# The last LayerNorm's scaling on ScalarE, the floor of the degrees on GpSimd, and a later store

## The chip, the cores and the metric

The kernel runs on one core of one Trainium2 chip. The metric is the device time of one execution in microseconds (us), as the median of seven. One further execution was taken with the hardware profiler; its page and its trace are what the text reads. Engines: PE is TensorE (PEld its weight loads), DVE is VectorE, ACT is ScalarE, POOL is GpSimd, SP is SyncE, which here only issues DMAs.

## What is computed

128 graphs of 128 nodes with 512 features each go through two layers. Layer 0 is graph attention with 8 heads of 64 features; layer 1 is a hypergraph convolution with a hidden width of 1024, a LayerNorm, and a second hypergraph convolution. Each layer adds its input and is followed by a LayerNorm without weights. The reference, cut to what matters:

```python
def _layernorm(x, axis=-1, eps=1e-5):
    m = jnp.mean(x, axis=axis, keepdims=True)
    v = jnp.var(x, axis=axis, keepdims=True)
    return (x - m) / jnp.sqrt(v + eps)

# layer 0, per graph and head
dense = leaky_relu(e_self[:, None] + e_neigh[None, :], 0.2) + NEG_BIG * (1.0 - A)
out = softmax(dense) @ feats + b          # heads side by side, then relu

# layer 1
def hypergraph_conv(x, adj, W, b):
    H = (adj != 0); w = adj.reshape(N, -1)[:, :C]
    xw = x @ W.T
    Dn = H @ w;         Dn = where(Dn > 0, 1 / Dn, 0)
    Be = H.sum(axis=1); Be = where(Be > 0, 1 / Be, 0)     # the degrees
    return Dn * (H @ (Be * (H.T @ xw))) + b
h = layer_norm(relu(hypergraph_conv(x, adj, W1, b1)), gamma, beta)
y = hypergraph_conv(h, adj, W2, b2) + x

x = _layernorm(x + layer0(x, adj))
x = _layernorm(x + layer1(x, adj))        # the last LayerNorm
```

## The kernel before

All arithmetic is in float32. Two graphs form a pair (index p, 64 pairs; g = 0, 1 within one), and most tiles hold both. A pair passes through five stages of one period each, so that five pairs are in work at a time. Every piece of work is a function registered with a lag (which period after the pair's start) and a time within a period of T = 38.6; the number `(p + lag) * T + time` is its place in one list. The list is sorted, and each engine and each DMA queue gets its instructions in this order[...]. For the first pairs a dictionary `first` sets places by hand, for the last two pairs there are others. The place numbers only order the work; real time is set by the engines.

The steps that the prediction speaks of, in the order of a pair:

- `edges` (L401, lag 0): DVE turns the adjacency block by block, makes the 0/1 matrix hT and sums its rows into deg (L411), takes the maximum of deg and 1 (L415) and the reciprocal (L416). deg has 2 numbers in each of the 128 partitions. `scale_edges` (L420, lag 1): DVE multiplies hT by the reciprocal into hB (L423). `propagator` (L428) multiplies hB and hT on PE, `r_evict` (L438) scales the result by the nodes' degrees into R (L440).
- `spread_rows` (L528): the neighbours' scores go from ft through DRAM (rd, L542); `neighbours` (L550, L560) spreads them to all partitions as nb (two loads of 512 KB), `spread_nodes` (L563, L566) the nodes' degrees as dnb.
- `masked` (L576, L579): POOL adds the mask to the scores, in four quarters; `leaky` (L583, L595) on ACT; `largest` (L597, L601) on DVE; `exponential` (L606, L609) on ACT. The exponentials go through DRAM to be transposed (L613, L621, L630), `attend` multiplies on PE, `attended`, `add_bias` (POOL, L691) and `residual` (DVE, L698) finish layer 0.
- The first LayerNorm: `moments` (L701) and `rstds` (L709) give mean (mv) and 1/sqrt (rs; vea and rsa for the first, veo and rso for the last LayerNorm), with the power on POOL (L714). `first_shift` (L727) makes -mean * rs on ACT in three small instructions (L730, L732), `first_output` (L737) scales on ACT with it (L739).
- `propagate` (pz on PE, L762), `z_evict` (ACT, zT, L774), `z_sums` (POOL, zS, L785), `hidden` (PE, ph, L797), with copies of partial products by ACT (L332); `h_sum`, `relu`, `square`, and `squares` (POOL, L850), which adds the squares of the hidden LayerNorm in three steps for each g; `h_sums` (POOL, hS, L458); `weigh` on PE (py, L476).
- The hidden LayerNorm's sums go through DRAM as well: `sum_blocks` (DVE), `write_sums` (SP, sd, L906), `read_sums` (SP, L912), `sum_rest` (DVE, L920, L922), `h_rstd` (POOL, L946 to L949, veh and rsh), `y_scale` (DVE, L953).
- `skip` (DVE, L750) starts o, `output` (PE, pq, L963), `o_sum` (DVE, L972), `o_stats` (DVE, L706), `rstds` with key "o"; `o_norm` (L984, lag 4, 17.0) calls `normalize` (L716), which takes (o - mean) * rs on DVE for each g (L717); `store` (L989, L990, lag 4, 19.5) writes o. o has two buffers.

SP issues nearly all DMAs of the steady part, in the order of the list. Around the store that is: the rows of x in blocks (L121), the store (L990), the adjacency in blocks (L129), rd (L542), nb (L560, twice), dnb (L566), sd (L906), the next rows of x (L112), the sums (L912, four), the next adjacency (L98, L104).

The very last pair has its own tail (`last_norm` and others, L994 to L1084), with its normalization on DVE.

Of the kernel before, what the change touches and what calls it, by code (L numbers as in the profile page):

```python
# [8 lines left out]
F32 = mybir.dt.float32  # L9
AF = mybir.ActivationFunctionType  # L10
ALU = mybir.AluOpType
# [9 lines left out]
def kernel(  # L21
# [45 lines left out]
    nc = tc.nc  # L67
    G, N, F = x.shape
    P = 128
# [15 lines left out]
    small = ctx.enter_context(tc.tile_pool(name="small", bufs=4))  # L85
# [114 lines left out]
    for i in range(2):  # L200
        t = const.tile([P, 2, H, UW + 1], F32, name=f"ft{i}")
# [99 lines left out]
    LAST = PAIRS - 1  # L301
    steps = []

    def step(lag, time, since=0, until=PAIRS):

        def keep(fn):
            steps.append((lag, time, fn.__name__, range(since, until), fn, ()))
            return fn
        return keep

    def at(lag, time, fn, *args, since=0, until=PAIRS):
        steps.append((lag, time, fn.__name__, range(since, until), fn, args))
# [87 lines left out]
    @step(0, 35.75)  # L400
    def edges(p, s):  # L401

        deg = small.tile([P, 2], F32, tag="deg", name=f"deg_{p}")
        hT = work.tile([P, 2, N], F32, tag="hT", name=f"hT_{p}")
        if p < 2:
            src = s["pt"][:, :2 * N].rearrange("p (g n) -> p g n", g=2)
        else:
            src = hT
            nc.vector.transpose(hT.rearrange("p g (b n) -> p (g b) n", b=NB), s["ab"])
        for g in range(2):  # L410
            nc.vector.tensor_scalar(  # L411
                hT[:, g, :], src[:, g, :], 0.0, None, op0=ALU.not_equal, op1=ALU.add,
                accum_out=deg[:, g:g + 1],
            )
        nc.vector.tensor_scalar(deg, deg, 1.0, None, op0=ALU.max)  # L415
        nc.vector.reciprocal(deg, deg)  # L416
        s["hT"], s["be"] = hT, deg

    @step(1, 10.8)
    def scale_edges(p, s):  # L420
        s["hB"] = work.tile([P, 2, N], F32, tag="hB", name=f"hB_{p}")
        for g in range(2):
            nc.vector.tensor_scalar(  # L423
                s["hB"][:, g, :], s["hT"][:, g, :], s["be"][:, g:g + 1], None, op0=ALU.mult
            )
# [287 lines left out]
        s["rs", key] = small.tile([P, 2], F32, tag="rs", name=f"rs{key}_{p}")  # L713
        nc.gpsimd.tensor_tensor(s["rs", key], ve, mhalf, op=ALU.pow)  # L714

    def normalize(s, key, t, g):  # L716
        nc.vector.tensor_scalar(  # L717
            t, t, s["mv", key][:, g, 0:1], s["rs", key][:, g:g + 1], op0=ALU.subtract,
            op1=ALU.mult,
        )  # L720

    at(2, 26.2, residual, 0)
    at(2, 30.7, residual, 1)
    at(2, 30.8, rstds, "a")

    @step(2, 33.12)
    def first_shift(p, s):  # L727
        s["sh"] = small.tile([P, 2], F32, tag="sh", name=f"sh_{p}")
        nm = small.tile([P, 2], F32, tag="nmean", name=f"nmean_{p}")
        nc.scalar.activation(nm, s["mv", "a"][:, :, 0], AF.Identity, scale=-1.0)  # L730
        for g in range(2):
            nc.scalar.activation(  # L732
                s["sh"][:, g:g + 1], nm[:, g:g + 1], AF.Identity,
                scale=s["rs", "a"][:, g:g + 1],
            )

    def first_output(p, s, g):  # L737
        t = s["y"][:, g, :]
        nc.scalar.activation(  # L739
            t, t, AF.Identity, bias=s["sh"][:, g:g + 1], scale=s["rs", "a"][:, g:g + 1]  # L740
        )

    at(2, 33.13, first_output, 0)
    at(2, 33.14, first_output, 1)

    def skip(p, s, g):
# [119 lines left out]
    def weigh(s, i, to, start):  # L866
# [3 lines left out]
          QU, 1, until=LAST)  # L870
# [109 lines left out]
    at(4, 15.5, o_stats, 1, until=LAST)  # L980
    at(4, 15.6, rstds, "o", until=LAST)

    @step(4, 17.0, until=LAST)
    def o_norm(p, s):  # L984
        for g in range(2):
            normalize(s, "o", s["o"][:, g, :], g)

    @step(4, 19.5, until=LAST)
    def store(p, s):  # L989
        nc.sync.dma_start(out[2 * p:2 * p + 2].rearrange("g n f -> n g f"), s["o"])  # L990

# [80 lines left out]
    for t, fn, *args in (  # L1072
# [40 lines left out]
        ("nodes", 0): 12.9, ("write_nodes", 0): 12.92, ("spread_nodes", 0): 15.9,  # L1113
        ("edges", 0): 14.46, ("edges", 2): 119.2,
        ("x_transpose", 2, 0): 120.5, ("x_transpose", 2, 1): 121.1, ("scale_edges", 0): 14.47, ("propagator", 0): 14.55,
        ("r_evict", 0): 99.76,
        ("spread_rows", 1): 15.72, ("nodes", 1): 15.55, ("write_nodes", 1): 15.85,
        ("edges", 1): 110.4, ("scale_edges", 1): 110.5, ("neighbours", 1): 80.1,
        ("propagator", 1): 117.76, ("spread_nodes", 1): 80.3, ("r_evict", 1): 121.8,
# [98 lines left out]
```

## Time and profile before

| | |
|---|---|
| median of 7 executions | 2461.6 us (2461.19 to 2462.88) |
| the profiled execution | 2461.45 us, of which the span from first to last instruction is 2459.4 us |
| granted PE clock | 0.998 |
| PE, steady part (200 to 2350 us) | busy 2146.84 of 2150 us |
| DMA | 345.30 MB, mean 140 GB/s |

In the steady part a pair takes some 37.6 us. Views of the profile used below: the page gives each engine's busy time and the share of the span; groups list instructions by line, engine and shapes ("xcount | busy us, mean ns | idle before"); waits list "engine line waited for <- releaser: us in total, times, longest"; timelines give start, length, engine, line, operation and, in brackets, the idle time before and what ended it. A busy PE is not a PE at its peak, and a wait is put down to what came last by the profile.

The groups that the change touches:

| line | what | count | mean |
|---|---|---|---|
| L717 | DVE, normalization of o, 128x512 | 126 | 772 ns |
| L415 | DVE, maximum of deg and 1, 128x2 | 64 | 996 ns |
| L416 | DVE, reciprocal of deg, 128x2 | 64 | 166 ns |
| L739 | ACT, scaling of the first LayerNorm, 128x512 | 128 | 799 ns |
| L730, L732 | ACT, its shifts, 128x2 and 128x1 | 64, 128 | 203, 287 ns |
| L990 | SP, the store, 512 KB | 63 | 407 ns to issue (median) |

### The profile page before, as it was taken

Reading aid. Unit: us, or ns where it says so; the run is one execution under the profiler, and the core shown is the slowest. Engines: PE = TensorE matmul, PEld = TensorE weight load, DVE = VectorE, ACT = ScalarE, POOL = GpSimd, SP = SyncE. Lnnn points to the kernel's source line nnn. Section 1 sums busy time; section 2 is a strip of 40 time slices with the busy share of each in tenths; the row PEclk is TensorE's granted clock in tenths of the full one; section 3 lists DMA queues with packets and bytes.
Section 4 is the critical chain, followed back from the end, with each engine's and each line's share of the span. In section 5 each row is a group of like instructions: output and inputs, shape, how many; then the busy total and the mean of one; then the engine's idle time right before and its main releaser. Section 6 shows DMA issues by size and latency. Waiting matters only on the chain.

```text
span 2459.4 us, 53018 instructions
## 1 busy us (share of the span) xinstructions
PE 2427.1 (99%) x18273; PEld 2148.7 (87%) x18273; DVE 2021.9 (82%) x4580; ACT 1532.3 (62%) x4481; POOL 1825.8 (74%) x2060
## 2 busy tenths in 40 slices
PE   7999999999999999999999999999999999999998
PEld 5888888888888888888888888888888888888897
DVE  7988888888888888888888888888888888888876
ACT  4665665755756656657557566566575665665763
POOL 5877777777777777777777777777777778777774
PEclk9999999999999999999999999999999999999999
DMA  6545445445454454454454544554545545545531
GB/s 183 142 141 144 146 132 154 143 128 152 140 141 144 142 144 145 130 155 141 130 153 139 142 144 143 146 145 129 152 142 133 151 138 144 143 140 150 144 111 52
DMA packets 432763, 345.30 MB, mean 140 GB/s; under 512 B 153176, under 2 KB 382064, under 8 KB 432496
## 3 DMA queue, kind: packets, MB, share of 16 engines
q1 hardware_dynamic: 429024, 337.46, 48.2%
q10 hardware_dynamic: 3472, 4.47, 0.5%
q8 instruction: 145, 2.38, 0.4%
q14 instruction: 122, 1.00, 0.1%
HBM read 239.08 MB, written 102.73 MB: 139 GB/s over the span
## 4 chain that ended last, share of the span: by engine, by line
PE 50%; DVE 19%; POOL 18%; ACT 6%; issue 4%; DMA 3%; SPq 0%; POOLq 0%; DVEq 0%; ACTq 0%
PE phX L797 10%; PE pyX L476 9%; POOL hS L458 6%; PE pfX L476 5%; PE phW L797 5%; PE pyW L476 5%; POOL zS L785 3%; POOL sq L850 3%; ACT nb L595 3%; PE pav L667 3%; PE pz L762 2%; PE phY L797 2%; DVE y L953 2%; PE pq L963 2%; PE pfW L476 2%
## 5 line engine op out<-in xcount | busy, mean ns | idle before, releaser
L797 PEld LDWEIGHTS phX<-zS,w_sb 128*128 128x128 f32 x3072 | 363.1, 192 | 33.0 <-issue 31.6
L332 ACT COPY py<-pyX 128x257 f32<-128x257 f32 x189 | 70.6, 374 | 506.6 <-PE pyX L476 503.9
L797 PE MATMUL phX<-zS,w_sb 128*128 128x128 f32 x3072 | 374.3, 275 | 2.4 <-POOL xS L458 1.3
L850 POOL TENSOR_TENSOR sq<-sq 128x512 f32<-128x512 f32 (+2 forms) x384 | 343.2, 894 | 20.1
L579 POOL TENSOR_TENSOR nb<-nb,neg 128x512 f32<-128x512 f32 x256 | 318.4, 1277 | 7.3 <-DMA nb<-rd 7.3
L609 ACT ACTIVATE nb<-nb,nm 128x128 f32<-128x128 f32 x1024 | 318.0, 391 | 8.1 <-DVE nm L601 8.1
L595 ACT ACTIVATE nb<-nb,ft 128x128 f32<-128x128 f32 x1020 | 317.2, 388 | 7.1 <-POOL nb L579 7.1
L714 POOL TENSOR_TENSOR rso<-veo,mhalf 128x2 f32<-128x2 f32 x63 | 44.1, 700 | 371.2 <-DVE veo L712 371.2
L827 ACT ACTIVATE h<-h,vecs 128x128 f32<-128x128 f32 x768 | 245.1, 392 | 55.2 <-DVE h L812 55.2
L601 DVE TENSOR_REDUCE nm<-nb 128x4 f32<-128x512 f32 x256 | 174.6, 682 | 113.2 <-ACT nb L595 101.3
L476 PE MATMUL pyX<-w_sb,hS 128*128 128x257 f32 x1008 | 245.6, 385 | 0.0
L476 PE MATMUL pyX<-w_sb,h 128*128 128x257 f32 x1008 | 239.4, 379 | 0.5 <-ACT py L332 0.5
L476 PE MATMUL pyW<-w_sb,hS 128*128 128x256 f32 x1008 | 238.7, 379 | 1.0 <-DVE y L881 1.0
L476 PEld LDWEIGHTS pyW<-w_sb,hS 128*128 128x128 f32 x1008 | 190.6, 189 | 29.0 <-POOL rsa L714 1.7
L476 PEld LDWEIGHTS pyX<-w_sb,hS 128*128 128x128 f32 x1008 | 185.8, 189 | 28.6
L691 POOL TENSOR_TENSOR y<-y,b_bc 128x512 f32<-128x512 f32 x128 | 163.2, 1275 | 61.6 <-DVE y L682 61.6
L476 PEld LDWEIGHTS pyX<-w_sb,h 128*128 128x128 f32 x1008 | 186.4, 190 | 25.5 <-ACT py L332 0.9
L698 DVE SCALAR_TENSOR_TENSOR y<-y,x 128x512 f32<-128x512 f32 x128 | 153.6, 1200 | 56.7 <-POOL y L691 55.1
L667 PEld LDWEIGHTS pav<-ft,eT 128*64 128x64 f32 x4096 | 130.0, 138 | 43.8 <-issue 41.9
L953 DVE SCALAR_TENSOR_TENSOR y<-y,rsh,bw_bc 128x512 f32<-128x512 f32 x126 | 148.6, 1217 | 21.1 <-POOL rsh L949 19.8
L630 DVE STREAM_TRANSPOSE eT<-eb 128x512 f32<-128x512 f32 x252 | 163.5, 687 | 0.3 <-DMA eb<-ed 0.2
L838 ACT ACTIVATE sq<-h 128x512 f32<-128x512 f32 x256 | 160.5, 628 | 2.1
(174 smaller groups left out, 5747.2 us busy)
## 6 DMA issues: line engine op xcount, KB each, us to landing
nb<-rd SPq DMA_DIRECT2D x127, 512.0 KB
ed<-nb SPq DMA_DIRECT2D x126, 512.0 KB
eb<-ed SPq DMA_DIRECT2D x504, 128.0 KB
x<-in_x_dram SPq DMA_DIRECT2D x64, 512.0 KB
out_dram<-o SPq DMA_DIRECT2D x63, 512.0 KB
xb<-in_x_dram SPq DMA_DIRECT2D x248, 128.0 KB
a<-in_adj_dram SPq DMA_DIRECT2D x64, 128.0 KB
w<-in_adj_dram SPq DMA_DIRECT2D x128, 64.0 KB
```

Of the source, the lines that this page charges most:

```text
L476: nc.tensor.matmul(to[:, :n], lhs[:, k, :], rhs[:, k, :n], start=bool(start) and k == 0, stop=(k == nk - 1), skip_group_check=True,)
L579: nc.gpsimd.tensor_tensor(t, t, neg[:, :, None, :].to_broadcast([P, NB, HH, B]), op=ALU.add)
L595: nc.scalar.activation(t, t, AF.Prelu, bias=s["ft"][:, g, h, 0:1], alpha=SLOPE)
L601: nc.vector.tensor_reduce(s["nm"][:, g, hs], scores(p, s, g, hs).rearrange("p b h j -> p h b j"), AX.XY, ALU.max, negate=True,)
L609: nc.scalar.activation(t, t, AF.Exp, bias=s["nm"][:, g, h:h + 1])
L630: nc.vector.transpose(s["eT"][:, g, hs, :].rearrange("p h (b i) -> p h b i", b=NB), s["eb", g][:, :, hs, :].rearrange("p b h j -> p h b j"),)
L667: nc.tensor.matmul(t[rows, h * (U + 1):(h + 1) * (U + 1)], s["eT"][:, g, q * HH + h, rows], s["ft"][:, g, q * HH + h, 2:], start=True, sto ...
L691: nc.gpsimd.tensor_tensor(s["y"][:, g, :], s["y"][:, g, :], b0_bc, op=ALU.add)
L797: nc.tensor.matmul(to[:, m * N:(m + 1) * N], w[:, k, m * P:(m + 1) * P], rhs[:, k, :], start=bool(start) and m == 0 and k == 0, stop=(k == ...
L827: nc.scalar.activation(dst[:, k, :], src[:, k, :], AF.Relu, bias=b1_sb[:, c:c + 1])
L850: nc.gpsimd.tensor_tensor(t[:, :n, :], t[:, :n, :], t[:, n:2 * n, :], op=ALU.add)
L953: nc.vector.scalar_tensor_tensor(t, t, s["rs", "h"][:, g:g + 1], bw_bc.rearrange("p (j c) -> p j c", j=2), op0=ALU.mult, op1=ALU.add,)
```

## The change

The normalization of o by the last LayerNorm (all pairs but the last) goes from DVE to ACT, in the form that the first LayerNorm has: three small instructions for the shift, then a scaling for each g. Its place goes from 17.0 to 21.3, 21.4 and 23.5 in the period, behind the last of the squares (21.2); the second half stands behind the copy of the features (23.4). The store goes from 19.5 to 28.5, behind rd, nb and dnb and ahead of sd. The maximum of the degrees and 1 becomes a step of its own on POOL (`least_degree`, lag 0, 36.0, and by hand for the first three pairs), in place; the reciprocal stays on DVE and moves from `edges` to the head of `scale_edges`.

```diff
--- before.py
+++ after.py
@@ -412,12 +412,15 @@
                 hT[:, g, :], src[:, g, :], 0.0, None, op0=ALU.not_equal, op1=ALU.add,
                 accum_out=deg[:, g:g + 1],
             )
-        nc.vector.tensor_scalar(deg, deg, 1.0, None, op0=ALU.max)
-        nc.vector.reciprocal(deg, deg)
         s["hT"], s["be"] = hT, deg
+
+    @step(0, 36.0)
+    def least_degree(p, s):
+        nc.gpsimd.tensor_scalar(s["be"], s["be"], 1.0, None, op0=ALU.max)
 
     @step(1, 10.8)
     def scale_edges(p, s):
+        nc.vector.reciprocal(s["be"], s["be"])
         s["hB"] = work.tile([P, 2, N], F32, tag="hB", name=f"hB_{p}")
         for g in range(2):
             nc.vector.tensor_scalar(
@@ -713,32 +716,30 @@
         s["rs", key] = small.tile([P, 2], F32, tag="rs", name=f"rs{key}_{p}")
         nc.gpsimd.tensor_tensor(s["rs", key], ve, mhalf, op=ALU.pow)
 
-    def normalize(s, key, t, g):
-        nc.vector.tensor_scalar(
-            t, t, s["mv", key][:, g, 0:1], s["rs", key][:, g:g + 1], op0=ALU.subtract,
-            op1=ALU.mult,
-        )
-
     at(2, 26.2, residual, 0)
     at(2, 30.7, residual, 1)
     at(2, 30.8, rstds, "a")
 
     @step(2, 33.12)
     def first_shift(p, s):
-        s["sh"] = small.tile([P, 2], F32, tag="sh", name=f"sh_{p}")
-        nm = small.tile([P, 2], F32, tag="nmean", name=f"nmean_{p}")
-        nc.scalar.activation(nm, s["mv", "a"][:, :, 0], AF.Identity, scale=-1.0)
+        shifts(p, s, "a")
+
+    def shifts(p, s, key):
+        sh = s["sh", key] = small.tile([P, 2], F32, tag="sh", name=f"sh{key}_{p}")
+        nm = small.tile([P, 2], F32, tag="nmean", name=f"nmean{key}_{p}")
+        nc.scalar.activation(nm, s["mv", key][:, :, 0], AF.Identity, scale=-1.0)
         for g in range(2):
             nc.scalar.activation(
-                s["sh"][:, g:g + 1], nm[:, g:g + 1], AF.Identity,
-                scale=s["rs", "a"][:, g:g + 1],
+                sh[:, g:g + 1], nm[:, g:g + 1], AF.Identity, scale=s["rs", key][:, g:g + 1]
             )
 
+    def shifted(s, key, t, g):
+        nc.scalar.activation(
+            t, t, AF.Identity, bias=s["sh", key][:, g:g + 1], scale=s["rs", key][:, g:g + 1]
+        )
+
     def first_output(p, s, g):
-        t = s["y"][:, g, :]
-        nc.scalar.activation(
-            t, t, AF.Identity, bias=s["sh"][:, g:g + 1], scale=s["rs", "a"][:, g:g + 1]
-        )
+        shifted(s, "a", s["y"][:, g, :], g)
 
     at(2, 33.13, first_output, 0)
     at(2, 33.14, first_output, 1)
@@ -980,12 +981,17 @@
     at(4, 15.5, o_stats, 1, until=LAST)
     at(4, 15.6, rstds, "o", until=LAST)
 
-    @step(4, 17.0, until=LAST)
-    def o_norm(p, s):
-        for g in range(2):
-            normalize(s, "o", s["o"][:, g, :], g)
-
-    @step(4, 19.5, until=LAST)
+    @step(4, 21.3, until=LAST)
+    def o_shift(p, s):
+        shifts(p, s, "o")
+
+    def o_norm(p, s, g):
+        shifted(s, "o", s["o"][:, g, :], g)
+
+    at(4, 21.4, o_norm, 0, until=LAST)
+    at(4, 23.5, o_norm, 1, until=LAST)
+
+    @step(4, 28.5, until=LAST)
     def store(p, s):
         nc.sync.dma_start(out[2 * p:2 * p + 2].rearrange("g n f -> n g f"), s["o"])
 
@@ -1113,7 +1119,8 @@
         ("nodes", 0): 12.9, ("write_nodes", 0): 12.92, ("spread_nodes", 0): 15.9,
         ("edges", 0): 14.46, ("edges", 2): 119.2,
         ("x_transpose", 2, 0): 120.5, ("x_transpose", 2, 1): 121.1, ("scale_edges", 0): 14.47, ("propagator", 0): 14.55,
-        ("r_evict", 0): 99.76,
+        ("r_evict", 0): 99.76, ("least_degree", 0): 14.465, ("least_degree", 1): 110.45,
+        ("least_degree", 2): 119.25,
         ("spread_rows", 1): 15.72, ("nodes", 1): 15.55, ("write_nodes", 1): 15.85,
         ("edges", 1): 110.4, ("scale_edges", 1): 110.5, ("neighbours", 1): 80.1,
         ("propagator", 1): 117.76, ("spread_nodes", 1): 80.3, ("r_evict", 1): 121.8,
```

## The prediction, made before the changed kernel had run

> **What bounds the kernel now.** I read the busy times of the page first, then the waits of the steady part (200 to 2350 us), then the timelines of ACT and PE over two neighbouring pairs. Two lines of the page:
>
> ```profile
> PE 2427.1 (99%) x18273; PEld 2148.7 (87%) x18273; DVE 2021.9 (82%) x4580; ACT 1532.3 (62%) x4481; POOL 1825.8 (74%) x2060
> PEclk9999999999999999999999999999999999999999
> ```
>
> PE has work all the time at full clock. Time can be lost only in the few places where it waits, and can be gained only there or in the ramp. The waits of the steady part, most of which concern other engines:
>
> ```profile
> POOL rso L714 <- DVE veo L712: 334.4, 57, 5.9
> POOL zS L785 <- ACT zT L774: 49.0, 57, 1.1
> PEld phX L797 <- ACT zT L774: 8.7, 29, 0.3
> ACT zT L774 <- PE pz L762: 8.3, 28, 0.3
> DVE so L920 <- DMA sums_out<-sd: 10.2, 12, 2.2
> ```
>
> The third line is PE's whole loss that is not its own issue: 0.3 us in every second pair. The timelines show why (start, length):
>
> ```profile
> 1224.28 0.59 ACT L774 COPY zT<-pz 128x512 f32<-128x512 f32 x1 [0.30 <-PE pz L762]
> ...
> 1261.20 1.11 ACT L774 COPY zT<-pz 128x512 f32<-128x512 f32 x2
> ...
> 1224.08 2.01 PE L797 MATMUL phX<-zT,w_sb 128*128 128x128 f32 x16
> ...
> 1261.83 2.05 PE L797 MATMUL phX<-zT,w_sb 128*128 128x128 f32 x16
> ...
> 1299.32 2.00 PE L797 MATMUL phX<-zT,w_sb 128*128 128x128 f32 x16
> ```
>
> From phX to phX the two intervals are 37.75 and 37.49 us, of which the tightest that PE alone would need is about 37.44. From the end of the second zT copy (1224.87) to the end of the next one (1262.31) is 37.44 too. That second interval is a loop without PE, and the chain of waits follows it: zT, POOL's zS sums and rsh, then DVE without a gap from L953 to veo (L712), POOL's rso, squares L850, hS L458 and bias L691, DVE's L698 and vea, POOL's rsa, ACT's first_output and leaky, zT. In the first pair zT waits 0.30 us for PE; in the next PE waits for zT. So a longer loop costs its extra once in two pairs (about 31 times), and a shorter one gives at most the 0.3 us back, 31 times: 9.3 us.
>
> [...]
>
> ```profile
> L415 DVE TENSOR_SCALAR deg<-deg 128x2 f32<-128x2 f32 x64 | 63.7, 996 | 2.2
> L353 DVE TENSOR_SCALAR dn<-dd 128x2 f32<-128x2 f32 x64 | 12.7, 198 | 2.2
> L717 DVE TENSOR_SCALAR o<-o,mvo,rso 128x512 f32<-128x512 f32 x126 | 92.3, 772 | 0.0
> L416 DVE RECIPROCAL deg<-deg 128x2 f32<-128x2 f32 x64 | 10.6, 166 | 2.2
> ```
>
> The same two-element operation takes 996 ns beside POOL's mask additions (L579) and 198 beside an idle POOL. [...]
>
> **Normalization from DVE to ACT.** DVE loses 2 x 772 = 1.54 us a pair. It stood at 1203.0 to 1204.5 in the pair of 1200; behind it DVE does L499 and then idles 1.16 us until ACT's pf copy, and 0.37 us for POOL's L691 at 1211.2. So DVE's own time there is worth nothing. But it held up POOL's squares, which are in the loop: L850 takes 0.795 us (256 wide) and 0.520 (128 wide) beside L717, against 0.73 for zS of the same 256 columns and 0.452 for the 128-wide sum of g = 1. Gain to the loop: 0.065 + 0.068 = 0.13 us. ACT gets one L730 (203 ns), two L732 (287) and two L739 (799), some 2.2 us with overlaps. It has the square until 1206.48 and the ft copy at 1207.74, then nothing until 1210.37. The shifts and the first half end near 1207.8 and may push the ft copy by 0 to 0.1 us; the second half is done by 1208.5. DVE's rows transpose that needs ft starts at 1209.16. Cost 0; without that idle time it would be up to 2.2 us a pair. The statistics are ready since 1202.1, so ACT waits for nothing.
>
> **Floor of the degrees, reciprocal.** DVE loses L415 (0.996) and, there, L416 (0.166). What follows is R (L440) and the score maxima L601, and the waits put 89.6 us of L601 down to ACT's leaky: DVE arrives earlier and waits, gain 0. On POOL the floor costs what L947, also a 128x2 tensor_scalar, does: 222 ns. It stands between the mask additions (end 1223.94) and zS (1224.94, after 1.00 us of idling for zT; 0.68 in the next pair), and deg is ready at 1220.4: cost 0 in the steady part. If that gap were gone, 0.3 us in the loop. The reciprocal moves into scale_edges, between L750 and L423, and there DVE is in the loop with no gap: 0.165 + 0.034 until the dependent L423 = +0.20 us. Bounds for the loop in all: +0.20 if the squares gain nothing, -0.1 if they gain twice what I read. Taken: 0.20 - 0.13 = +0.07, x 31 = **+2.2 us** (-3 to +6.2).
>
> **The ramp.** The hand-made times of the first pairs put least_degree(2) at 119.25, on POOL between the second zS sum of pair 0 (119.2) and the third (119.9). In the trace:
>
> ```profile
> 57.25 0.73 POOL L785 TENSOR_TENSOR zS<-zT 128x256 f32<-128x256 f32 x1
> 57.94 0.73 POOL L785 TENSOR_TENSOR zS<-zT,zS 128x256 f32<-128x256 f32 x1
> 58.63 1.27 POOL L579 TENSOR_TENSOR nb<-nb,neg 128x512 f32<-128x512 f32 x1
> ...
> 61.91 1.27 ACT L595 ACTIVATE nb<-nb,ft 128x128 f32<-128x128 f32 x4
> 63.08 0.57 ACT L332 COPY ph<-phX 128x512 f32<-128x512 f32 x1
> ```
>
> DVE finishes the degrees of pair 2 at 60.67. POOL, in order, would stand from 57.3 to then. Behind it are two sums and the last mask addition of pair 1: 60.75 + 0.30 + 0.73 + 0.69 + 1.27 = 63.7. ACT's leaky of that quarter moves from 61.91 to 63.75, and behind it in ACT's order the copy of ph, for which PE waits already (63.79): +1.84 us. Earlier, least_degree(1) stands on POOL behind two mask additions (to 52.59), where DVE now has L423 at 50.18; L423, two short L423 against POOL's third addition, then L237: DVE is 0.4 to 0.8 us later, of which 0.45 reaches the degrees of pair 2. Sum **+2.3 us**; 0 if the later waits of the ramp (PE waits 1.00 us at 91.5 and 0.66 at 95.9) swallow it, 3 at most. The floor of pair 0 stands before a 6 us idle stretch of POOL: 0.
>
> **The store.** SP around it, in a usual pair:
>
> ```profile
> 1129.73 0.41 SPq L990 DMA_DIRECT2D out_dram<-o  x1
> ...
> 1135.66 0.94 SPq L560 DMA_DIRECT2D nb<-rd x2
> ```
>
> SP's later issues there: dnb 1136.65, sd 1140.85, x 1141.23, sums_out 1144.99. The store, 512 KB, moves behind dnb and so ahead of sd, x and the reading of the sums. SP itself has 3.7 us free between dnb and sd, so 0.41 us of issuing costs nothing. In the queue the store puts its transfer before sd: 1.4 us at the 300 GB/s seen at 1144 to 1145, 3 us if shared. DVE takes the sums at 1149.08, just as they land; POOL needs veh only after zS, 3.5 us later, 3.0 after DVE's two instructions. Behind L920 on DVE stand one L601 and the h sum L812, which begins 3.7 us later. Cost 0 in the usual pair. Some pairs are short of slack (in the pair of 1200 the wait at L920 is already 1.4 us, and sd took 5.1 us instead of 3.3): I take **+1 us** in all (0 to 5). nb stays ahead of the store; the o buffer is next written 19 us later.
>
> **Sum.** The profiled execution took 2461.45 us (span 2459.4, 2.05 around it), 0.15 below the median. 2461.45 + 2.2 + 2.3 + 1 = 2466.95, say **2467**. Its own range is 2462 to 2473.
>
> **Rivals.**
> - The loop shortens (not slower): [...] the net loop is 0.3 us shorter. PE's wait disappears: 2461.45 - 9.3 + 2.3 = 2454.5. It ends faster by more than a measurement can tell once the loop is 0.24 us shorter. [...] Against: the squares at 1239.82 show only the 0.13.
> - The store decides (slower): sd lands more than 3.0 us later and the sums hold up veh, DVE's L953 and the loop in each pair. At 0.5 us over, x 60 pairs: 2462 + 30 = 2492. For it: a store beside others took some 3 us, and L920 has no slack of its own. Against: 1.4 us at full rate and 3 us of slack to veh.
> - Nothing measurable: ramp swallowed, loop even: 2462.
>
> **How the numbers follow.** Forecast 0.52, shorter loop 0.15, store 0.17, nothing 0.16. About 0.2 % (4.9 us) is what can be told from no change here. A third of the forecast's case lies within it, all of the last: faster 0.15, same 0.34, slower 0.51. The range takes the forecast's own, the last rival, a third of the first and half of the store's: 2457 to 2477.
>
> **What would show it.** PE's wait for zT: 8.7 us now, about 11 by my sum, gone if the first rival is right. L850 at 0.73 and 0.45 behind rso; L423 0.2 us later after L750; POOL idle from 57.3 to 60.7 and PE's phX at 65.6 instead of 63.79; L920 waiting in most pairs but rsh never behind it. I am wrong if PE waits for y of L953 (store), or if ACT's ft copy or py copies come late.

## The result, and the profile after

The changed kernel takes 2467.7 us in the median (2464.9 to 2470.6, 15 runs), against 2461.6 of the kernel before (35 runs beside them): a ratio of 1.0024, with an interval of 1.0017 to 1.0031, so 6.1 us more. The prediction was 2467.0, in a range of 2457 to 2477. The profiled execution took 2468.29 us (span 2465.8), against 2461.45 (2459.4). From L415 on the lines have other numbers: rso is L717, the skip L751, zT L775, phX L798, the sums L921, the store L996.

The page's line of busy times, changed kernel:

```profile
PE 2432.9 (99%) x18273; PEld 2148.9 (87%) x18273; DVE 1871.8 (76%) x4390; ACT 1653.2 (67%) x4796; POOL 1828.1 (74%) x2124
```

150 us of work left DVE, 121 came to ACT, and the time grew. Neither engine's sum says anything about the end; PE is still at 99 %. The waits of the steady part (200 to 2350 us) of the changed kernel, with "us in total, times, longest":

```profile
POOL rso L717 <- DVE veo L715: 345.8, 57, 6.1
...
DVE so L921 <- DMA sums_out<-sd: 61.4, 53, 3.4
...
PEld phX L798 <- ACT zT L775: 8.2, 29, 0.5
ACT zT L775 <- PE pz L763: 5.7, 28, 0.3
...
PEld pfX L479 <- POOL rso L717: 3.5, 18, 0.4
...
POOL veh L947 <- DVE veh L923: 0.8, 2, 0.5
```

Three things are to be seen. DVE now waits for the hidden LayerNorm's sums in nearly every pair (12 times before, 53 now): that is the later store. POOL, behind it, waited only twice. And PE has a second short wait beside the one for zT, at pfX, which was not there before. Its named releaser is no operand of pfX; the second product of pfX goes into the bank that ACT copies just before. In the pair of 2073 this copy ends at 2073.05, and pfX's weight load starts at 2073.17. PE's two rows make 11.7 us together, where one row had 8.7.

The loop without PE, at its two altered places. DVE's timeline around the reciprocal, first two lines of the kernel before, then the changed kernel (start, length):

```profile
1232.02 1.82 DVE L750 SCALAR_TENSOR_TENSOR o<-y,b_bc 128x512 f32<-128x512 f32 x2
1233.76 0.47 DVE L423 TENSOR_SCALAR hB<-hT,deg 128x128 f32<-128x128 f32 x2
```

```profile
1235.95 1.81 DVE L751 SCALAR_TENSOR_TENSOR o<-y,b_bc 128x512 f32<-128x512 f32 x2
1237.69 0.15 DVE L423 RECIPROCAL deg<-deg 128x2 f32<-128x2 f32 x1
1237.88 0.48 DVE L426 TENSOR_SCALAR hB<-hT,deg 128x128 f32<-128x128 f32 x2
```

Before, the hB instructions started 1.74 us after the start of the two at L750; now 1.93. The tile view of the squares on POOL, in a stretch of one pair, before and then changed (minimum, median and maximum in ns):

```profile
L850 POOL TENSOR_TENSOR sq<-sq x3: 520/795/1271, 1239.8 to 1242.0; 128x512 f32<-128x512 f32 x1, 128x256 f32<-128x256 f32 x1, 128x128 f32<-128x128 f32 x1
L851 POOL TENSOR_TENSOR sq<-sq x3: 457/727/1275, 1243.9 to 1246.1; 128x512 f32<-128x512 f32 x1, 128x256 f32<-128x256 f32 x1, 128x128 f32<-128x128 f32 x1
```

The 128-wide square went from 520 to 457 ns, the 256-wide from 795 to 727. To see how typical the two places are, I took medians over pairs 8 to 51 from the start and end times in the traces, here with three of the experiments below:

| us | before | change | floor alone | change without floor | reciprocal apart |
|---|---|---|---|---|---|
| end of the second skip (L750) to the start of hB | -0.08 | 0.11 | 0.11 | -0.08 | -0.08 |
| squares, end of the first to end of the third | 1.47 | 1.34 | 1.47 | 1.35 | 1.35 |
| two pairs, from zT to zT | 75.21 | 75.29 | 75.46 | 75.12 | 75.14 |

(-0.08: in the trace the hB instruction begins 0.08 us before the one ahead of it ends.) Every other link of the loop agrees between before and change to 0.02 us, but for the last one, where zT waits for PE.

ACT, where the scaling went (timeline, changed kernel):

```profile
1209.79 0.63 ACT L839 ACTIVATE sq<-h 128x512 f32<-128x512 f32 x1
1210.32 0.19 ACT L730 ACTIVATE nmeano<-mvo 128x2 f32<-128x2 f32 x1
1210.61 0.48 ACT L732 ACTIVATE sho<-nmeano,rso 128x1 f32<-128x1 f32 x2
1210.99 0.80 ACT L737 ACTIVATE o<-o,sho,rso 128x512 f32<-128x512 f32 x1
1211.70 0.37 ACT L500 COPY ft<-pfX 128x264 f32<-128x264 f32 x1
1211.96 0.81 ACT L737 ACTIVATE o<-o,sho,rso 128x512 f32<-128x512 f32 x1
1214.32 0.37 ACT L332 COPY py<-pyX 128x257 f32<-128x257 f32 x1 [1.54 <-PE pyX L479]
```

The last line carries the point: after the new work ACT still waits 1.54 us for PE before the copy of py. The copy of ft, whose coming late the prediction named as a sign of being wrong, had waited 1.26 us for PE before and now does not wait; over pairs 8 to 51 it starts 0.05 us after pfX in the median, against 0.04 before, and at most 0.33. The new work just fits in there.

The ramp. POOL's timeline of the changed kernel:

```profile
56.62 0.73 POOL L786 TENSOR_TENSOR zS<-zT,zS 128x256 f32<-128x256 f32 x1
60.76 0.21 POOL L419 TENSOR_SCALAR deg<-deg 128x2 f32<-128x2 f32 x1 [3.41 <-DVE hT L411]
60.93 0.73 POOL L786 TENSOR_TENSOR zS<-zT 128x256 f32<-128x256 f32 x1
```

and PE's, first two lines of the kernel before, then the changed one:

```profile
63.79 2.02 PE L797 MATMUL phX<-zS,w_sb 128*128 128x128 f32 x16 [1.15 <-ACT ph L332]
67.07 2.02 PE L797 MATMUL phX<-zS,w_sb 128*128 128x128 f32 x16 [1.25 <-POOL xS L458]
```

```profile
65.50 3.47 PE L798 MATMUL phX<-zS,w_sb 128*128 128x128 f32 x16 [2.80 <-ACT ph L332]
69.70 2.02 PE L798 MATMUL phX<-zS,w_sb 128*128 128x128 f32 x16 [0.72 <-issue]
```

POOL stands for 3.41 us, as foretold, and keeps to the list: the zS behind the floor, whose zT ACT had finished at 55.74, begins at 60.93 instead of 57.25. PE's phX comes at 65.50 instead of 63.79. But that phX then takes 3.47 us for 16 matmuls that took 2.02 before. The windows view of PE has the reason in its granted clock, the number behind the count of matmuls (stretch, us, PE busy and matmuls, clock, DMA share, GB/s); before, this stretch had 34 matmuls at 1.00:

```profile
65.00:70.00 5.00, 3.77 (x19) 0.66 0.65 210
60.00:65.10 5.10, 2.70 (x25) 1.00 0.26 103
65.20:68.50 3.30, 3.00 (x14) 0.50 0.59 159
68.60:70.00 1.40, 0.68 (x7) 1.00 0.93 375
```

The 0.66 is a mean over 5 us: the narrower stretches show full clock until about 65.1, half of it until about 68.5, and full clock again. In the trace's own clock records the half lasts 3.41 us, from 65.13 to 68.54.

Setting each matmul of the changed kernel against the same one of before gives PE's lag, the time by which it runs behind: 1.70 us at 63.8 us, 3.16 at the end of the slow phX, 2.62 at 67.1, 2.16 from 91.5 on, then 2.75 by the fourth pair, 3.57 at pair 20, 4.67 at pair 40, 6.33 at the last. The last part is an even growth of about 2.5 us and two jumps, 0.44 at pair 35 and 0.65 at pair 51.

### The profile page after: what moved, and what is told of

Same layout as the page of the kernel before. It is cut to its first block, busy times and chain, and to the rows that moved or that the text cites. A ratio compares the mean times of both kernels' runs of the same rounds, so it can differ in the third digit from the quotient of the medians.

```text
span 2465.8 us, 53329 instructions
## 1 busy us (share of the span) xinstructions
PE 2432.9 (99%) x18273; PEld 2148.9 (87%) x18273; DVE 1871.8 (76%) x4390; ACT 1653.2 (67%) x4796; POOL 1828.1 (74%) x2124
## 4 chain that ended last, share of the span: by engine, by line
PE 59%; DVE 14%; POOL 12%; DMA 7%; ACT 6%; issue 2%; SPq 0%; POOLq 0%; DVEq 0%; ACTq 0%
PE phX L798 13%; PE pyX L479 9%; PE phW L798 6%; PE pfX L479 6%; PE pyW L479 5%; POOL hS L461 4%; PE phY L798 3%; PE pq L964 3%; ACT nb L598 3%; PE pav L670 3%; DMA nb<-rd 3%; PE pfW L479 3%; PE pz L763 3%; POOL zS L786 2%; PE pyY L479 2%; DMA sd<-sr 2%
## 5 line engine op out<-in xcount | busy, mean ns | idle before, releaser
L798 PEld LDWEIGHTS phX<-zS,w_sb 128*128 128x128 f32 x3072 | 364.6, 193 | 34.1 <-issue 30.3
L798 PE MATMUL phX<-zS,w_sb 128*128 128x128 f32 x3072 | 375.8, 276 | 3.5 <-ACT ph L332 2.8
L851 POOL TENSOR_TENSOR sq<-sq 128x512 f32<-128x512 f32 (+2 forms) x384 | 335.3, 873 | 23.2 <-ACT sq L839 3.0
L717 POOL TENSOR_TENSOR rso<-veo,mhalf 128x2 f32<-128x2 f32 x63 | 44.1, 700 | 383.4 <-DVE veo L715 383.4
L954 DVE SCALAR_TENSOR_TENSOR y<-y,rsh,bw_bc 128x512 f32<-128x512 f32 x126 | 148.6, 1217 | 19.6 <-POOL rsh L950 19.5
```

The source lines that it names most:

```text
L798: nc.tensor.matmul(to[:, m * N:(m + 1) * N], w[:, k, m * P:(m + 1) * P], rhs[:, k, :], start=bool(start) and m == 0 and k == 0, stop=(k == ...
L851: nc.gpsimd.tensor_tensor(t[:, :n, :], t[:, :n, :], t[:, n:2 * n, :], op=ALU.add)
```

## The experiments

Differences are to the kernel before, run beside each experiment on the same chip (2461.8 to 2462.8 us).

### The change in two halves

Without the floor's part (the maximum and the reciprocal back in `edges` on DVE; scaling and store as changed):

```diff
+        nc.vector.tensor_scalar(deg, deg, 1.0, None, op0=ALU.max)
+        nc.vector.reciprocal(deg, deg)
         s["hT"], s["be"] = hT, deg
-    @step(0, 36.0)
-    def least_degree(p, s):
...
-        nc.vector.reciprocal(s["be"], s["be"])
```

> The change without the floor: normalization on ACT and the store at 28.5 as in the change, the degrees as before. Loop theory: DVE's L717 no longer holds up POOL's squares, the loop is 0.13 us shorter, PE's wait for zT shrinks by as much 31 times (-4.0 us), late pairs cost +1.1, the ramp is as before: 2461.6 - 4.0 + 1.1 = 2458.7 us. Rival, ACT is the cost (its 2.2 us a pair more make its copies late): slower than before, most of the change's +6.1, about 2466. Rival, the store is the cost: about 2467.

Measured: 2459.3 us (21 runs), -3.3; ratio 0.9987 (0.9980 to 0.9993).

The floor's part alone, put into the kernel before with its places of the first pairs:

```diff
-        nc.vector.tensor_scalar(deg, deg, 1.0, None, op0=ALU.max)
-        nc.vector.reciprocal(deg, deg)
+    @step(0, 36.0)
+    def least_degree(p, s):
+        nc.gpsimd.tensor_scalar(s["be"], s["be"], 1.0, None, op0=ALU.max)
...
+        nc.vector.reciprocal(s["be"], s["be"])
```

> The floor of the degrees on POOL and the reciprocal in scale_edges alone; normalization and store as before. Loop theory: the reciprocal makes the loop 0.20 us longer (x 31 = +6.2) and the ramp costs +2.7: 2461.6 + 8.9 = 2470.5 us, slower than the whole change. Rivals (ACT or the store is the cost): 2461 to 2464.

Measured: 2471.7 us (5 runs), +9.1; ratio 1.0037 (1.0024 to 1.0049). The halves add up to +5.8, against +6.1 for the change. So the scaling on ACT is a gain, through the squares on POOL (1.47 us before, 1.35 without the floor's part, in the table), and the floor with its reciprocal is the whole loss. In the table above each half alters its own place and not the other's. The rivals that put a cost on ACT (2466) or on the store (2467) are refuted for the first half.

### The floor of the first three pairs back on DVE

```diff
+        if p < 3:
+            nc.vector.tensor_scalar(deg, deg, 1.0, None, op0=ALU.max)
+            nc.vector.reciprocal(deg, deg)
-    @step(0, 36.0)
+    @step(0, 36.0, since=3)
     def least_degree(p, s):
...
+        if p >= 3:
+            nc.vector.reciprocal(s["be"], s["be"])
```

> The change, but floor and reciprocal of the first three pairs stay on DVE in edges as before. Theory of the ramp: POOL no longer stands from 57.3 to 60.7, PE's phX starts at 63.8 again, the time falls by the 2.7 us that the pairs lay behind after the fourth: 2467.7 - 2.7 = 2465.0 us. Rival, the later waits of the ramp would have swallowed it: 2467.7, as the change.

Measured: 2466.1 us (21 runs), +3.5; ratio 1.0015 (1.0008 to 1.0021). That is 2.6 less than the change. PE waits 1.11 us before the phX of 64.19, which takes 2.02 us, and the clock is 1.00 from 65 to 70 us. The difference fits the 2.7 that were expected, though 2466.1 itself is 1.1 above the expected 2465.0. The trace is less even: counted from 62 us, just ahead of the pause, PE's lag at the fourth pair is 0.6 us where the change has 2.7, so 2.1 less; from there to the last pair it grows by 4.3 where the change's grows by 3.6, and why is open. So the pause of POOL in the ramp costs some 2 us; whether by being a pause or by the clock, this run can't tell.

### The pause of PE filled

The 16 matmuls of the first pair that run just before the pause are done twice, so that PE works through most of it. The second pass writes the same values to the same bank, which is read 7 us later.

```diff
             multiply(s, i, s[kind, where], start)
+            if kind == "ph" and p == 0 and i == 5:
+                multiply(s, i, s[kind, where], start)
```

> The change, with the 16 matmuls phW of the first pair (60.75 to 62.70 us in the profile of the change) done twice, so that TensorE works through most of its pause before phX at 65.50; the second pass writes the same values to the same bank, whose reader comes at 69.63. Nothing else moves. Theory: the pause of 2.80 us made the granted clock fall (0.66 from 65 to 70 us, phX 3.47 us instead of 2.02), and with the pause filled it stays at 1.00: phX takes 2.02 us, the next phX starts at about 68.3 instead of 69.70, and TensorE is some 1.3 us behind the kernel before there and 0.3 to 1.3 us at the second pair's pz instead of 2.16. Time 0.9 to 1.9 us below that of the change, about 2466.3. Rival: the clock does not depend on the pause, or waits behind it swallow what it cost: the lag at the second pair stays at 2.2 us and the time at 2467.7.

> The changed kernel itself, as the base for the run with the filled pause on the same chip. Both theories: 6.1 us above the kernel before, about 2467.7, clock 0.66 from 65 to 70 us again, phX near 3.5 us.

Measured: 2465.7 us (21 runs), +3.9; ratio 1.0015 (1.0009 to 1.0022). The change beside it: 2467.8 us (9 runs), +6.0; ratio 1.0026 (1.0016 to 1.0036). PE's timeline with the pause filled:

```profile
61.15 3.74 PE L800 MATMUL phW<-zS,w_sb 128*128 128x128 f32 x32
65.85 2.02 PE L800 MATMUL phX<-zS,w_sb 128*128 128x128 f32 x16 [0.97 <-ACT ph L334]
68.63 2.02 PE L800 MATMUL phX<-zS,w_sb 128*128 128x128 f32 x16 [0.76 <-issue]
```

phX starts as late as in the change, but PE had stood for 0.97 us only, and the same 16 matmuls take 2.02 us (clock 1.00 from 65 to 70 us; 0.70 in the change beside it, where phX takes 3.38). Each trace has a lag of its own ahead of the pause (at 62 us 0.45 us here, 0.05 in the change). Counted from there it is 1.11 us at 67.1 us and 0.65 at the second pair's pz, where the change has 2.58 and 2.12: 1.47 us less at both. With 16 matmuls more on the busiest engine the median is 2.1 us lower (20 of its 21 runs lie below the fastest of the nine of the change; the two intervals against the kernel before overlap, so the size is taken from the trace). The rival is refuted: 1.5 of the ramp's 2.2 us were the clock, and the waits behind them swallowed none of it.

### The reciprocal out of the loop

The reciprocal of the change becomes a step of its own, ten units of the period earlier.

```diff
+    @step(1, 0.3)
+    def invert_degree(p, s):
+        nc.vector.reciprocal(s["be"], s["be"])
+
     @step(1, 10.8)
     def scale_edges(p, s):
-        nc.vector.reciprocal(s["be"], s["be"])
```

> The change, but the reciprocal is a step of its own at place 0.3 of the period, where DVE is about to wait for the sums, and no longer between L750 and L423. Loop theory: the loop loses the 0.19 us again, x 31 = -5.9: 2467.7 - 5.9 = 2461.8 us. Rival, the reciprocal is hidden and the loss in the steady part has another cause (the store's queueing, ACT): 2467 to 2468.

Measured: 2461.9 us (13 runs), -0.7; ratio 1.0000 (0.9992 to 1.0008). The ramp is as in the change (lag 2.76 at the third pair), but from there the lag falls to 0.63 at the last pair, since the loop keeps only the gain at the squares. Two pairs take 0.15 us less than in the change (table), x 31 = 4.7 us; the two jumps of the change's lag, 1.1 us, are gone too. So the loop itself gave less than the 5.9 that were expected, and the two together what was measured. PE's wait at pfX is gone as well, and the one for zT is 6.4 us. That second wait needs the reciprocal, then, but not the reciprocal alone: the floor alone has no row for pfX (PE loses its time at zT there, 13.4 and 3.7 us), and with the store at 33.0 the row has 0.2 us.

### The whole scaling of the edges out of the loop

If 0.20 us in this place cost so much, the 0.47 us of the two hB instructions, which were there before, should be worth removing. In the kernel before, only their place is changed:

```diff
-    @step(1, 10.8)
+    @step(1, 0.3)
     def scale_edges(p, s):
...
+        ("scale_edges", 2): 126.6,
```

> The kernel before with one step moved: scale_edges from 10.8 to 0.3, before DVE takes the sums, no work added or left out. Loop theory: DVE is without it between L750 and L972, the loop is 0.39 us shorter, more than the 0.3 us of PE's wait: 2461.6 - 9.3 = 2452.3 us. Rival, PE's wait for zT is not made by this loop: 2461 to 2462.

Measured: 2452.1 us (5 runs), -9.7; ratio 0.9959 (0.9946 to 0.9973). DVE's timeline of that kernel and two of its waits (200 to 2350 us):

```profile
1219.12 0.48 DVE L423 TENSOR_SCALAR hB<-hT,deg 128x128 f32<-128x128 f32 x2
...
1226.90 1.81 DVE L750 SCALAR_TENSOR_TENSOR o<-y,b_bc 128x512 f32<-128x512 f32 x2
```

```profile
PEld phX L797 <- issue: 27.4, 114, 0.2
...
ACT zT L774 <- PE pz L762: 17.9, 58, 0.3
```

hB is done 7 us before the loop comes by. PE's wait for zT is gone from the list, and zT waits for PE in all 58 pairs, not in every second one. Two pairs take 74.87 us (medians as above), twice the 37.44 that the prediction gave as PE's own least: the loop has let go of PE, and 31 x (75.21 - 74.87) = 10.5 us.

With the change's scaling on ACT, the store behind the reading of the sums (33.0), the floor back on DVE, and `scale_edges` at 0.3:

> Normalization on ACT, the store at 33.0, floor and reciprocal on DVE in edges as before, and scale_edges moved from 10.8 to 0.3 (pair 2 at its old place). Loop theory: the loop loses 0.13 and 0.39 us, more than PE's wait for zT, which disappears: 2461.6 - 9.3 = 2452.3 us. Rival, another wait takes its place: 2456 to 2462.

Measured: 2451.7 us (5 runs), -10.1; ratio 0.9960 (0.9948 to 0.9973). Both are faster than the two kernels of this case, and the intervals don't tell them apart: once the loop is off PE, the scaling on ACT adds nothing that can be measured.

### The store

In the change, the store behind the reading of the sums:

```diff
-    @step(4, 28.5, until=LAST)
+    @step(4, 33.0, until=LAST)
     def store(p, s):
```

> The change with the store at 33.0, behind the reading of the sums. Theory: sd lands 1.2 us earlier again, the two pairs in which rsh had to wait for the sums lose nothing: 2467.7 - 1.1 = 2466.6 us. Rival, the store's place is the main cost: 2462 or less.

Measured: 2467.6 us (9 runs), +5.8; ratio 1.0026 (1.0016 to 1.0035). From the issue of sd to the first reading of the sums, the medians by the trace are 4.14 us before, 5.37 in the change and 3.91 here. DVE's wait for the sums shrinks from 61.4 us to 5.2, and POOL's row for veh is gone, as are the two jumps of the lag. The time hardly moves: the store is not where the 6 us come from. The 1 us that it was given is shown by the jumps in the trace, and is too small for these times to resolve. The same move made in the version without the floor:

> Normalization on ACT with the store at 33.0, behind the reading of the sums; floor, reciprocal and scale_edges as before. Loop theory: the loop is 0.12 us shorter and no pair waits for late sums: 2461.6 - 3.7 = 2457.9 us, 1 us below the run with the store at 28.5. Rival, the store's place costs nothing that can be seen: 2459.3 as there.

Measured: 2458.6 us (20 runs), -4.1; ratio 0.9984 (0.9978 to 0.9991), against -3.3 with the store at 28.5. Right by size, and again not told apart by the intervals.

How far is the store from harm? First I doubled it:

```diff
-        nc.sync.dma_start(out[2 * p:2 * p + 2].rearrange("g n f -> n g f"), s["o"])
+        for _ in range(2):
+            nc.sync.dma_start(out[2 * p:2 * p + 2].rearrange("g n f -> n g f"), s["o"])
```

> The change with the store issued twice in a row at its place, the same 512 KB to the same rows of the output. Theory: sd lands another 1.2 us later (some 6.5 us after its issue); in the change's trace 17 of the 62 pairs have less than that to spare before POOL takes the sums, together 9 us; some of it is swallowed: 2467.7 + 5 to 9 = 2473 to 2477 us. Rival, the queue holds no more than the store already showed (SP is blocked instead): below 2470.

Measured: 2540.0 us (5 runs, one of which took 4188 us and is not in the ratio), +78; ratio 1.0312 (1.0297 to 1.0326). A miss, and the experiment's fault. SP's timeline of that kernel, and its wait (200 to 2350 us):

```profile
1213.96 9.69 SPq L997 DMA_DIRECT2D out_dram<-o  x2
1223.74 0.72 SPq L907 DMA_DIRECT2D sd<-sr  x1
```

```profile
SPq L997 <- DMA out_dram<-o: 391.1, 56, 8.7
```

Both stores write the same rows, and in this program SP waits at the second until the first has landed. It stood some 7 us per pair, and sd behind it was issued late. This measures a blocked queue, not a second transfer. So a second transfer of the same size to other memory, added to the work:

```diff
         nc.sync.dma_start(out[2 * p:2 * p + 2].rearrange("g n f -> n g f"), s["o"])
+        s["o2"] = dram.tile([2, P, F], F32, tag="o2", name=f"o2_{p}")
+        nc.sync.dma_start(s["o2"].rearrange("g n f -> n g f"), s["o"])
```

> The change with a second transfer of 512 KB behind the store, to rows of a scratch area in DRAM that nothing reads, so that it waits for no earlier one. Theory of the queue: SP goes on at once, sd lands another 1.2 us later (some 6.5 us after its issue), and the pairs that have less than that to spare before POOL takes the sums lose the rest: 2467.7 + 5 to 9 = 2473 to 2477 us. Rival, what made the doubled store slow was the queue itself: again 2530 or more.

Measured: 2489.1 us (4 runs), +26.3; ratio 1.0108 (1.0091 to 1.0125). Again a miss: 5 to 9 us above the change were expected, and it is some 20. Two of its waits (200 to 2350 us):

```profile
DVE so L921 <- DMA sums_out<-sd: 148.3, 57, 5.8
...
POOL veh L947 <- DVE veh L923: 22.9, 22, 2.9
```

The reading of the sums is issued 7.15 us after sd in the median, 1.8 later than in the change, where I had put 1.2. POOL now waits for them in 22 listed cases, for 22.9 us, about the 20 us by which the time is above the change's. Other waits grew with it (DVE's R for the transfer of dnb from 7.2 to 18.9 us, and PE waits 9.4 us for POOL's xS, a row that the change has not), so the 20 us can't all be put down to the sums. The prediction's second rival is thus a real mechanism: at some 3 us of delay over the kernel before, where the prediction put its edge, POOL waits in a third of the pairs; the change itself uses 1.2 us. No run places the edge more closely, and none tells whether sd stands behind the big transfer in the queue or shares the DMA engines with it.

## Why the prediction was right

**The loop.** The reciprocal was put at +0.20 us: the table has 0.19, and 0.01 more before L973. The squares were put at -0.13, and gained 0.13. Net +0.07 was predicted and +0.08 measured, x 31 = 2.5 us against 2.2; the even growth of PE's lag is 2.5. The floor alone shows the first number without the second: 75.46 - 75.21 = 0.25 us in two pairs, some 7.5 us from the fourth pair to the last; its lag grows by 7.3 there. I expected all of it in PE's row for zT, "about 11". That row stayed at 8.2, and 3.5 us stand in the new row at pfX; the way over ACT's copy of pf was not foreseen. That the two rows make 11.7 is no proof of the sum: in the second trace of the change they make 10.4 (9.0 and 1.4), though two pairs take as long there (75.31 us) and PE's lag grows as much, by 2.6 us besides its jumps. The size of the loop's loss rests on those two, not on the rows.

**The ramp: the size right, the steps wrong.** +2.3 was predicted, 1.84 for the pause and 0.45 for degrees of pair 2 that come later. 2.16 us are in PE's lag at the second pair, and 2.75 by the fourth, with 0.6 lost between 108 and 134 us that also appear where the floor of the first pairs is on DVE (0.6 in that trace), so not from the pause. The step "ACT's leaky moves from 61.91 to 63.75, and behind it the copy of ph" is confirmed: 63.62, and phX 1.70 us later. Three other steps failed. The 0.45 did not come: DVE is 0.5 us behind at 55.4, but its wait of 0.47 us before the next maximum (L601) takes that up, and the transpose for pair 2 starts at 59.70 in both kernels. The delay of 1.7 us was carried to the end whole, but about 1 us of it was taken up by waits that were there anyway, half at the phX of 67.07, which had waited 1.25 us for POOL's sums, and half at 91.5, the wait that the prediction named and then did not use. In place of both came the clock, which the prediction left out: the filled pause shows 1.5 us. 1.7 - 1.0 + 1.5 = 2.2. The errors cancelled; that the ramp's size came out right was luck.

**The clock in the ramp.** In the change half the clock (0.50) was granted for 3.41 us, from 65.13, which is 2.43 us after PE's last matmul ahead of the pause, to 68.54. Over 65 to 70 us the clock was 0.67 behind a pause of 2.44 us (floor alone), 0.66 and 0.70 behind 2.80 and 2.89 (change, twice), 0.66 behind 2.74 and 2.82 (later store, reciprocal apart), and 1.00 behind 1.79 (second transfer) and 1.15 (before). With the store doubled, behind 2.72 us, the first five matmuls of phX took 1.41 us, where sixteen take 2.02 at full clock. An earlier pause, 7.17 us from 44.2 on, is in both kernels: there the half was granted from 47.96 to 54.78 us before, and from 44.65 to 54.89 in the change. So after pauses of the same length it neither began at the same time nor lasted as long. No run has a pause here between 1.79 and 2.44 us, and none shows what sets the fall besides the pause.

**The store.** +1 was predicted; the two jumps make 1.1 us, and POOL's only two waits for veh are 0.8 us; in the second trace of the change it is 0.7 us in two jumps, and 0.5 in the waits. That the jumps are those waits is read from the trace, and supported by their absence with the later store; the times alone can't show it. One number of the prediction is off: 512 KB at 300 GB/s take 1.7 us, not 1.4. Nor is that a full rate: 309 GB/s is what was moved from 1144 to 1145 us, and the changed kernel shows 375 above. The sums were read 1.2 us later, inside the 3 us that the usual pair has to spare. That the store's transfer would go ahead of sd's in the queue was my assumption, and is not shown. SP's wait until 1144.99, where it issues the reading of the sums, is no sign of it: SP issued x at 1141.23 in between, and what waits until then is the reading of sd's own rows (190.6 us in 58 waits for sd before).

**ACT and DVE.** Cost 0 for the scaling on ACT, gain 0 for DVE's 150 us: the version without the floor is faster by 3.3 us and its loop is shorter by the squares alone (75.12). The floor on POOL costs nothing in the loop either, as predicted: with the reciprocal apart it is still on POOL, and two pairs take 75.14.

**The rivals.** A shorter loop needed 0.24 us; the change is on the other side of zero, and the scaling of the edges moved out shows what that rival would have given. The store decides only with twice the transfers.

## What to carry to other kernels

Before moving work off an engine, find the loop that has no slack and count only what lies in it: here 150 us less work for DVE were worth only the 3 us that they took off POOL's squares, and 0.15 us of a two-element reciprocal in the wrong place cost 6 us. When such a place is found, look at what else stands in it; moving 0.47 us of older work out of it gave 9.7 us. In a ramp, follow a delay through the next waits instead of adding it to the end, and look at what clock PE is granted behind the pause: here, behind 2.80 us, half of it for 3.41 us.

## What the hardware showed that I had not expected

- Behind a pause of PE of 2.4 to 2.9 us in the ramp the granted clock was 0.66 to 0.70 from 65 to 70 us, in the change 0.50 for 3.41 us of it; 16 matmuls took 3.3 to 3.6 us instead of 2.02. Filling the pause with 16 repeated matmuls took 1.5 us off PE's lag.
- With one 512 KB store issued ahead of the 16 KB of sd, the sums were read 5.37 us after the issue of sd instead of 4.14, with a second such transfer 7.15.
- In this program, two stores to the same rows, issued in a row, made SP stand some 7 us between them (391.1 us in 56 waits). No run here shows whether it has to wait there.
